# The first chunk of an expert FFN, worked tile by tile as its rows are gathered

## The chip, the cores and the metric

One NeuronCore of one Trainium2 chip runs the kernel. The metric is the device time of a launch in microseconds (us); before the change it is 1994.89 us, the median of 3 runs (1994.32 to 1996.13). Engines are called TensorE (matmuls; in the profile PE, and PEld for its weight loads), VectorE (DVE), ScalarE (ACT), GpSimd (POOL) and SyncE (SP, which here only starts DMAs).

## The reference, cut to what matters

The layer is a "macaron": half an expert FFN, an attention, half an expert FFN again, over 8192 tokens of width 256, all in float32.

```python
x = x + 0.5 * ffn(layernorm(x), router_w, wg, wu, wd)
x = x + attn(layernorm(x), Wq, bq, Wk, bk, Wv, bv, Wo, bo)
x = x + 0.5 * ffn(layernorm(x), router_w, wg, wu, wd)
```

In the FFN each token goes to its two best of 8 experts. An expert takes at most 1280 tokens (those of highest weight), and computes for its gathered rows `disp` (unused places are rows of zeros):

```python
g = einsum('ecd,edf->ecf', disp, wg)
u = einsum('ecd,edf->ecf', disp, wu)
eo = einsum('ecf,efd->ecd', silu(g) * u, wd)     # D = 256, F = 1024
```

The results, weighted, are added back to the tokens' rows. The change touches only how the first gathered rows of each FFN reach the first products.

## The kernel before, in words

The program runs four stages in order: the first router (which norms the rows, chooses experts and writes the rows with their weights to DRAM), the first FFN (`experts`, from L452), attention with the second router, and the second FFN (`experts` again). In both FFNs the code is the same.

**Chunks.** An expert's 1280 places are worked in two chunks of 640, each made of `CH` = 5 tiles of 128 rows; an FFN has 16 chunks. For each chunk, `gather` (L464) starts five indirect DMAs from GpSimd's queue, each bringing a tile `r` of 128 rows. `blank` (L477) multiplies a tile by 0 or 1 per row, on ScalarE, or on VectorE for tiles 1 and 3 of chunk 0. `turn` (L487) transposes one half of the width (`c`, 0 or 1) of tiles 0 to 2 or of tiles 3 and 4 into the PSUM bank `tr`, and ScalarE copies the bank to `xsT`; four calls (`q` = 0 to 3: c 0 tiles 0-2, c 0 tiles 3-4, c 1 tiles 0-2, c 1 tiles 3-4) turn a chunk.

**Products.** The first and second matrices of the expert, `wg` (m = 0) and `wu` (m = 1), are multiplied by a Strassen-like scheme: the inner width of 256 is split in two (c), the 640 columns in two halves of `BH` = 320, the 1024 outputs in two halves, and seven products of 128x128 weights with 320 columns replace eight, for each of `NF` = 4 groups `p` of outputs. `sums_of_x` (L544) makes the four sums of column blocks that the scheme needs (`xs`), on VectorE; `sums_of_w` and `sum_of_wd` make those of the weights. A product's result takes a pair of PSUM banks (`banks`, tag `mm`, three pairs in rotation), one bank for m = 0 and one for m = 1. Each float32 matmul in the code is two instructions on TensorE in the profile; a transpose is one.

For one p: the first product (block 11 of the weights by block 11 of x) is copied by ScalarE to `p1`; the second product is added to it in PSUM (for p = 0 of chunk 0 it goes to a pair of its own, and VectorE adds the two into block 0 of `ct`); the sixth product, added to `p1`, gives `u2` (u in the profile), and the following products lead to the other blocks. Then SiLU, the multiplication of the two halves, and in `down` (L749) the third matrix.

**Order.** The stage runs under a schedule written by hand: on TensorE, VectorE and ScalarE the instructions run in the order in which the code emits them. Only GpSimd's order is left to the planner. In the middle of an FFN a chunk's blanks and turns are placed between the products of the chunk before it. The first chunk has none before it, and its start is written out: after the list of rows is made (`first`, L835 to L843), `gather(0)`, `gather(1)`, the sums of the weights on VectorE, then blanks of tiles 0 to 2, turns 0 and 2, blanks of tiles 3 and 4 (L848 to L851), and then, in `units(0)` (L559), the first product, turn 1, half the second product, turn 3, the other half (L623 to L631), the four sums of x, and the addition of the two products (L633). After that come the sum of `wd` (L635), the sixth product with the addition that makes u (L610 to L615, L636), another sum of `wd`, and the loop over p.

The lines in the profile that matter here: L471 the gathers, L483 and L485 the blanks, L496 transposes, L499 copies to `xsT`, L502 all VectorE additions by `tt` (told apart by their tiles: xs, ct, u, wds, ws), L570 the products, L607 the copy to p1.

Of the kernel before, what the change touches and what calls it, by code (L numbers as in the profile page):

```python
# [8 lines left out]
F32 = mybir.dt.float32  # L9
# [4 lines left out]
ALU = mybir.AluOpType  # L14
# [4 lines left out]
P = 128  # L19
# [7 lines left out]
def macaron_kernel(  # L27
# [22 lines left out]
    nc = tc.nc  # L50
    B, N, D = x_in.shape
# [3 lines left out]
    DC = D // P  # L55
# [3 lines left out]
    CH = 5  # L59
    BANK = 512  # L60
# [21 lines left out]
    ident = const.tile([P, P], F32, name="ident")  # L82
# [353 lines left out]
    def load_expert(e, wpool, weights):  # L436
        if e >= E:
            return
        wgt = wpool.tile([P, DC, F], F32, tag="wgt", name="wgt")
        wut = wpool.tile([P, DC, F], F32, tag="wut", name="wut")  # L440
        wdt = wpool.tile([P, FC, D], F32, tag="wdt", name="wdt")
        nc.sync.dma_start(out=wgt, in_=wg[e].rearrange("(c p) f -> p c f", p=P))
        nc.sync.dma_start(out=wut, in_=wu[e].rearrange("(c p) f -> p c f", p=P))
        nc.sync.dma_start(out=wdt, in_=wd[e].rearrange("(f p) d -> p f d", p=P))
        weights[e] = wgt, wut, wdt
# [3 lines left out]
    BH = CH * P // 2  # L449
    TURN = 3  # L450

    def experts(name, src, dst, wait_for, weights, wpool, pool, ppool):  # L452
# [8 lines left out]
        lists, got, xTs, turned, ws, wds, xs = {}, {}, {}, {}, {}, {}, {}  # L461
        sent = {-1: list(wait_for)}

        def gather(k):  # L464
            if k >= len(chunks):
                return
            e, i0 = chunks[k]
            got[k] = []
            for i in range(i0, i0 + CH):
                r = pool.tile([P, W], F32, tag="r", name="r", bufs=10)  # L470
                nc.gpsimd.indirect_dma_start(  # L471
                    out=r, out_offset=None, in_=src[:, :],
                    in_offset=bass.IndirectOffsetOnAxis(ap=lists[e][:, i : i + 1], axis=0),
                )
                got[k].append(r)

        def blank(k, *tiles):  # L477
            for i in tiles:
                if k < len(chunks):
                    e, r = chunks[k][0], got[k][i]  # L480
                    has = r[:, D + E + e : D + E + e + 1]
                    if k == 0 and i % 2:
                        nc.vector.tensor_scalar(r[:, 0:D], r[:, 0:D], has, None, ALU.mult)  # L483
                    else:
                        nc.scalar.mul(r[:, 0:D], r[:, 0:D], has)  # L485

        def turn(k, q):  # L487

            if k >= len(chunks):
                return  # L490
            if q == 0:
                turned[k] = xTs[k] = pool.tile([P, DC, CH * P], F32, tag="xsT", name="xsT", bufs=2)
            c, i0, i1 = q // 2, (0, TURN)[q % 2], (TURN, CH)[q % 2]
            ps = ppool.tile([P, BANK], F32, tag="tr", name="tr", bufs=1)
            for i in range(i0, i1):
                nc.tensor.transpose(  # L496
                    ps[:, (i - i0) * P : (i - i0 + 1) * P], got[k][i][:, c * P : (c + 1) * P], ident
                )
            nc.scalar.copy(turned[k][:, c, i0 * P : i1 * P], ps[:, : (i1 - i0) * P])  # L499

        def tt(o, a, b, op):
            nc.vector.tensor_tensor(o, a, b, op)  # L502

# [3 lines left out]
        def sums_of_w(e, m):  # L507

            if e >= E:
                return  # L510
            if m == 0:
                ws[e] = pool.tile([P, 2, 4, FH], F32, tag="ws", name="ws", bufs=1)
            v, o = weights[e][m], ws[e]
            a11, a12, a21, a22 = v[:, 0, :FH], v[:, 1, :FH], v[:, 0, FH:], v[:, 1, FH:]
            tt(o[:, m, 0, :], a21, a22, ALU.add)
            tt(o[:, m, 1, :], o[:, m, 0, :], a11, ALU.subtract)
            tt(o[:, m, 2, :], a11, a21, ALU.subtract)
            tt(o[:, m, 3, :], a12, o[:, m, 1, :], ALU.subtract)

        def sum_of_wd(k, j):  # L520


            if k % PER:
                return
            e = chunks[k][0]
            v = weights[e][2]
            if j == 0:
                wds[e] = pool.tile([P, 4, NF, P], F32, tag="wds", name="wds", bufs=1)
            o = wds[e]
            a11, a12, a21, a22 = v[:, :NF, :P], v[:, NF:, :P], v[:, :NF, P:], v[:, NF:, P:]  # L530
            of = ((a21, a22, ALU.add), (o[:, 0], a11, ALU.subtract), (a11, a21, ALU.subtract),
                  (a12, o[:, 1], ALU.subtract))
            tt(o[:, j], *of[j])
# [10 lines left out]
        def sums_of_x(k):  # L544
            if k >= len(chunks):
                return
            v = turned.pop(k)
            o = xs[k] = pool.tile([P, 4, BH], F32, tag="xs", name="xs", bufs=1)
            b11, b12, b21, b22 = v[:, 0, :BH], v[:, 0, BH:], v[:, 1, :BH], v[:, 1, BH:]
            tt(o[:, 0, :], b12, b11, ALU.subtract)  # L550
            tt(o[:, 1, :], b22, o[:, 0, :], ALU.subtract)
            tt(o[:, 2, :], b22, b12, ALU.subtract)
            tt(o[:, 3, :], b21, o[:, 1, :], ALU.subtract)

        def banks():

            return ppool.tile([P, 2, BANK], F32, tag="mm", name="mm", bufs=3)

        def units(k):  # L559
            e = chunks[k][0]  # L560
            xT, hs = xTs.pop(k), []

            def product(p, m, ps, j, c, b, start=True):


                if c is None:
                    a = ws[e][:, m, j, p * P : (p + 1) * P]
                else:
                    a = weights[e][m][:, c, j * FH + p * P : j * FH + (p + 1) * P]
                nc.tensor.matmul(ps, a, b, start=start, stop=True, skip_group_check=not start)  # L570

            def both(p, *what):
                ps = banks()
                for m in range(2):
                    product(p, m, ps[:, m, :BH], *what)
                return ps[:, :, :BH]
# [8 lines left out]
            cts, firsts, sixths, u2s = {}, {}, {}, {}  # L585
# [7 lines left out]
            def block(p, q):  # L593

                return cts[p][:, :, q, :]
# [7 lines left out]
            def first_product(p):  # L603

                ps = both(p, 0, 0, xT[:, 0, :BH])
                p1 = pool.tile([P, 2, BH], F32, tag="p1", name="p1", bufs=1)
                nc.scalar.copy(p1, ps)  # L607
                firsts[p] = ps, p1
# [8 lines left out]
            def second_product(p):  # L617
                cts[p] = pool.tile([P, 2, 4, BH], F32, tag="ct", name="ct", bufs=NF)
                c11 = onto(p, firsts.pop(p)[0], 0, 1, xT[:, 1, :BH])
                nc.scalar.activation(h(p)[:, 0, :], c11[:, 0, :], AF.Silu)  # L620
                nc.scalar.copy(hT(p)[:, 0, :], c11[:, 1, :])

            first_product(0)  # L623
            if k == 0:

                turn(0, 1)
                cts[0] = pool.tile([P, 2, 4, BH], F32, tag="ct", name="ct", bufs=NF)
                ps = banks()
                product(0, 0, ps[:, 0, :BH], 0, 1, xT[:, 1, :BH])
                turn(0, 3)  # L630
                product(0, 1, ps[:, 1, :BH], 0, 1, xT[:, 1, :BH])  # L631
                sums_of_x(0)
                tt(block(0, 0), firsts[0][1], ps[:, :, :BH], ALU.add)  # L633
            x4 = xs.pop(k)
            sum_of_wd(k, 0)  # L635
            sixth_product(0)  # L636
            sum_of_wd(k, 1)
            if k > 0:
                second_product(0)
            send(k - 1, 2, 3)  # L640
            for p in range(NF):
                last = p == NF - 1
                u2, ps = u2s.pop(p), sixths.pop(p)
# [192 lines left out]
        with tc.manual_schedule(engines=ENGINES - {mybir.EngineType.Pool}):  # L836
            first.high()
            first.begin()
            for g in range(NL):
                first.low(g)  # L840
                first.products(g)
            first.sum()
            lists[0] = first.end()  # L843
            gather(0)
            gather(1)
            for m in range(2):
                sums_of_w(0, m)
            blank(0, *range(TURN))  # L848
            for q in (0, 2):
                turn(0, q)  # L850
            blank(0, *range(TURN, CH))  # L851
            for k, (e, i0) in enumerate(chunks):
                (down if k < len(chunks) - 1 else down_at_once)(k, units(k))
                if i0 + CH == ST:
                    load_expert(e + 2, wpool, weights)
# [379 lines left out]
    with tc.tile_pool(name="w1", bufs=2) as wpool:  # L1235
        weights = {}
        with tc.tile_pool(name="r1", bufs=1) as pool, tc.tile_pool(name="r1p", bufs=2, space=PSUM) as ppool:
# [5 lines left out]
            with tc.manual_schedule(engines=ENGINES):  # L1243
                nc.gpsimd.memset(wrx, 0.0)
                ps = ppool.tile([P, DC, P], F32, tag="turn", name="wrT", bufs=1)
# [4 lines left out]
                ps = ppool.tile([P, DC, P], F32, tag="turn", name="means", bufs=1)  # L1250
# [74 lines left out]
```

## Time and profile before

| | us |
|---|---|
| median of 3 runs | 1994.89 |
| the profiled execution | 1995.5 |
| its span, first to last instruction | 1993.6 |
| TensorE busy with matmuls | 1832.5 (92%) |
| VectorE busy | 1408.0 (71%) |
| GpSimd busy | 1024.0 (51%) |
| ScalarE busy | 957.9 (48%) |
| mean granted TensorE clock | 0.957 of full |

In the views that follow, times are in us from the first instruction. The chain is followed back from the last instruction, at each step to what released it. "Idle before" is the time in which an engine had nothing running ahead of the instruction, with what ended it. An engine's rows overlap slightly[...]. The first FFN's first tile is blanked at 117.19, the second FFN's at 1205.06.

### The profile page before, as it was taken

To read this page: it belongs to the slowest core of one execution; us is meant where nothing else is said; L and a number is where in the kernel's file an instruction comes from. 1 tells how busy PE (TensorE), PEld (TensorE's weight loads), DVE (VectorE), ACT (ScalarE), POOL (GpSimd) and SP (SyncE) were. 2 spreads that over 40 slices of the span, in tenths; PEclk is the share of its full clock that TensorE was granted. 3 is DMA by queue.
4 is the path that set the end of the run, shared out by engine and by line. 5 is a ranking of instruction groups with operands and counts; after the bars stand their busy time and mean duration, and the time that the engine had idled before them with its cause. 6 is when DMAs were issued, how large, how long until landed. Compare 5 with 4: busy or idle time off the path is not lost.

```text
span 1993.6 us, 25454 instructions
## 1 busy us (share of the span) xinstructions
PE 1832.5 (92%) x8756; PEld 1333.5 (67%) x8756; DVE 1408.0 (71%) x2609; ACT 957.9 (48%) x2373; POOL 1024.0 (51%) x1036
## 2 busy tenths in 40 slices
PE   6369999999999999999999617999999999999998
PEld 4247777777777777777888415777777777777776
DVE  8866767676767676646788886676767676666763
ACT  5435454555546463325455404555546463736332
POOL 5325555555555555535555304555555555555552
PEclk8579999999999999999999858999999999999999
DMA  9901313232222221125012541222222222231121
GB/s 348 318 28 28 91 28 91 37 82 66 53 70 49 70 49 28 28 25 172 22 43 87 173 152 29 50 69 70 49 70 49 70 49 71 49 91 31 31 30 19
DMA packets 99936, 147.67 MB, mean 74 GB/s; under 512 B 7512, under 2 KB 86368, under 8 KB 99680
## 3 DMA queue, kind: packets, MB, share of 16 engines
q1 hardware_dynamic: 69072, 102.77, 15.1%
q0 software_dynamic: 30720, 43.27, 13.5%
q8 instruction: 69, 1.13, 0.2%
q14 instruction: 59, 0.48, 0.1%
q10 hardware_dynamic: 16, 0.01, 0.0%
HBM read 98.84 MB, written 55.57 MB: 77 GB/s over the span
## 4 chain that ended last, share of the span: by engine, by line
PE 82%; DVE 8%; issue 1%; POOL 1%; ACT 1%; DMA 1%; POOLq 0%; DVEq 0%; ACTq 0%; SPq 0%
PE mm L570 48%; PE mm L770 23%; PE tr L496 2%; PE back L722 2%; PE pc L1012 1%; PE qp L957 1%; PE ix L413 1%; PE py L1070 1%; DVE above L309 1%; PE mm L828 1%; DVE st L1082 1%; DVE xw L1080 1%; DVE q L965 1%; DVE m L970 0%; DVE z L979 0%
## 5 line engine op out<-in xcount | busy, mean ns | idle before, releaser
L570 PE MATMUL mm<-xs,ws 128*128 128x320 f32 x1536 | 477.0, 433 | 3.9 <-DVE u L502 3.0
L505 POOL TENSOR_TENSOR ct<-ct 128x320 f32<-128x320 f32 x360 | 338.8, 941 | 188.8 <-DVE ct L601 165.3
L570 PEld LDWEIGHTS mm<-xs,ws 128*128 128x128 f32 x1536 | 284.3, 190 | 113.0 <-DVE u L502 4.1
L502 DVE TENSOR_TENSOR ct<-u,mm 128x640 f32<-128x640 f32 x256 | 209.8, 820 | 180.4 <-PE mm L570 168.0
L502 DVE TENSOR_TENSOR ct<-ct,mm 128x640 f32<-128x640 f32 x288 | 235.9, 819 | 74.3 <-PE mm L570 74.1
L598 ACT ACTIVATE ct<-ct 128x960 f32<-128x960 f32 (+2 forms) x192 | 141.7, 738 | 297.9 <-DVE ct L502 297.9
L471 POOL DMA_INDIRECT r<-rows,ixs x160 | 157.8, 986 | 236.0 <-ACT eo L703 172.9
L770 PE MATMUL mm<-ct,wds 128*128 128x320 f32 x960 | 278.1, 432 | 0.0
L407 ACT ACTIVATE lo<-from_below,behind_lo 128x129 f16<-128x129 f32 x896 | 272.9, 395 | 0.0
L770 PEld LDWEIGHTS mm<-ct,wds 128*128 128x128 f32 x960 | 178.6, 190 | 72.8 <-DVE ct L502 6.0
L770 PE MATMUL mm<-ct,wdt 128*128 128x320 f32 x720 | 213.5, 433 | 0.0
L704 POOL DMA_INDIRECT out_dram<-eo,ixs x80 | 127.6, 1595 | 142.1 <-ACT eo L703 124.5
L704 POOL DMA_INDIRECT acc<-eo,ixs x80 | 127.6, 1595 | 141.9 <-ACT eo L703 124.0
L570 PE MATMUL mm<-xsT,wgt 128*128 128x320 f32 x512 | 183.4, 440 | 0.0
L570 PE MATMUL mm<-xsT,wut 128*128 128x320 f32 x512 | 180.7, 435 | 0.0
L601 DVE TENSOR_TENSOR ct<-ct 128x640 f32<-128x640 f32 (+1 forms) x128 | 165.7, 1295 | 18.7 <-ACT ct L598 18.7
L502 DVE TENSOR_TENSOR u<-p,mm 128x640 f32<-128x640 f32 x128 | 105.1, 821 | 88.2 <-PE mm L570 81.0
L770 PEld LDWEIGHTS mm<-ct,wdt 128*128 128x128 f32 x720 | 132.1, 190 | 47.5
L607 ACT COPY p<-mm 128x640 f32<-128x640 f32 x128 | 88.3, 690 | 154.5 <-PE mm L570 154.5
L570 PE MATMUL mm<-xsT,ws 128*128 128x320 f32 x512 | 158.7, 432 | 0.0
L703 ACT ACTIVATE eo<-back,r 128x256 f32<-128x256 f32 x150 | 65.0, 478 | 152.4 <-PE back L722 152.4
L570 PEld LDWEIGHTS mm<-xsT,wut 128*128 128x128 f32 x512 | 97.7, 191 | 40.7 <-issue 0.8
(226 smaller groups left out, 2836.9 us busy)
## 6 DMA issues: line engine op xcount, KB each, us to landing
wgt<-in_L_ffn_wg_dram SPq DMA_DIRECT2D x16, 1024.0 KB, 4.9
wut<-in_L_ffn_wu_dram SPq DMA_DIRECT2D x16, 1024.0 KB, 6.9
wdt<-in_L_ffn_wd_dram SPq DMA_DIRECT2D x16, 1024.0 KB, 5.3
rows<-xw SPq DMA_DIRECT2D x7, 2176.0 KB, 10.7
xw<-in_L_attn_x_dram SPq DMA_DIRECT2D x16, 512.0 KB, 8.2
out_dram<-xw SPq DMA_DIRECT2D x16, 512.0 KB, 2.9
xw<-acc SPq DMA_DIRECT2D x15, 512.0 KB, 8.8
r<-rows,ixs POOLq DMA_INDIRECT x160, 2.8
```

The source lines that it names most:

```text
L407: nc.scalar.activation(lo[:, t, :], from_below, AF.Sign, bias=at, scale=1.0)
L471: nc.gpsimd.indirect_dma_start(out=r, out_offset=None, in_=src[:, :], in_offset=bass.IndirectOffsetOnAxis(ap=lists[e][:, i : i + 1], axis=0),)
L496: nc.tensor.transpose(ps[:, (i - i0) * P : (i - i0 + 1) * P], got[k][i][:, c * P : (c + 1) * P], ident)
L502: nc.vector.tensor_tensor(o, a, b, op)
L505: nc.gpsimd.tensor_tensor(o, a, b, op)
L570: nc.tensor.matmul(ps, a, b, start=start, stop=True, skip_group_check=not start)
L598: nc.scalar.activation(h(p)[:, qs, :], h(p)[:, qs, :], AF.Silu)
L601: engine.tensor_tensor(h(p)[:, qs, :], h(p)[:, qs, :], hT(p)[:, qs, :], ALU.mult)
L607: nc.scalar.copy(p1, ps)
L703: nc.scalar.mul(eo, ps, got[k][i][:, D + e : D + e + 1])
L704: ins = nc.gpsimd.indirect_dma_start(out=dst[:, :], out_offset=bass.IndirectOffsetOnAxis(ap=lists[e][:, i0 + i : i0 + i + 1], axis=0), in_ ...
L770: nc.tensor.matmul(ps, a(p), b(p), start=(p == 0 and not more), stop=(p == NF - 1), skip_group_check=more)
```

## The change

For chunk 0 alone, the order is turned round. Each of the five tiles is blanked, then transposed whole: both halves of its width go into the one `tr` bank by two transposes, and one ScalarE copy of 256 columns takes them to `xsT` (`turn_tile`). As soon as a tile is there, its columns are multiplied: of the first 320 columns, tile 0 gives 128, tile 1 gives 128 and tile 2 gives 64, and for each of these groups the first product (c = 0, into `ps`) and the second product (c = 1, into `ps2`, a pair of banks of its own) are made, both for m = 0 and 1. After tile 2, ScalarE copies `ps` to `p1`. Tiles 3 and 4 are only blanked and turned. The sums of x stand after all five tiles. The addition of the two products into block 0 moves behind the sixth product, its addition u, and the second sum of `wd`. Other chunks are as before.

```diff
+        def turn_tile(k, i):
+            ps = ppool.tile([P, BANK], F32, tag="tr", name="tr", bufs=1)
+            for c in range(DC):
+                nc.tensor.transpose(ps[:, c * P : (c + 1) * P], got[k][i][:, c * P : (c + 1) * P], ident)
+            nc.scalar.copy(
+                turned[k][:, :, i * P : (i + 1) * P], ps[:, :D].rearrange("p (c s) -> p c s", c=DC)
+            )
...
-            xT, hs = xTs.pop(k), []
+            xT, hs = turned[0] if k == 0 else xTs.pop(k), []
...
-            first_product(0)
             if k == 0:
 
-                turn(0, 1)
                 cts[0] = pool.tile([P, 2, 4, BH], F32, tag="ct", name="ct", bufs=NF)
-                ps = banks()
-                product(0, 0, ps[:, 0, :BH], 0, 1, xT[:, 1, :BH])
-                turn(0, 3)
-                product(0, 1, ps[:, 1, :BH], 0, 1, xT[:, 1, :BH])
+                ps, ps2 = banks(), banks()
+                for i in range(CH):
+                    blank(0, i)
+                    turn_tile(0, i)
+                    at = slice(i * P, min((i + 1) * P, BH))
+                    for c, o in ((0, ps), (1, ps2)) if i < TURN else ():
+                        for m in range(2):
+                            product(0, m, o[:, m, at], 0, c, xT[:, c, at])
+                    if i == TURN - 1:
+                        p1 = pool.tile([P, 2, BH], F32, tag="p1", name="p1", bufs=1)
+                        nc.scalar.copy(p1, ps[:, :, :BH])
+                        firsts[0] = None, p1
                 sums_of_x(0)
-                tt(block(0, 0), firsts[0][1], ps[:, :, :BH], ALU.add)
+            else:
+                first_product(0)
             x4 = xs.pop(k)
             sum_of_wd(k, 0)
             sixth_product(0)
             sum_of_wd(k, 1)
-            if k > 0:
+            if k == 0:
+                tt(block(0, 0), p1, ps2[:, :, :BH], ALU.add)
+            else:
                 second_product(0)
...
-            blank(0, *range(TURN))
-            for q in (0, 2):
-                turn(0, q)
-            blank(0, *range(TURN, CH))
+            turned[0] = pool.tile([P, DC, CH * P], F32, tag="xsT", name="xsT", bufs=2)
```

## The prediction

> **What bounds the kernel now.** I read the page first, then the chain that ended last in order of time, then the order of time at the two places that the change touches, then windows that show TensorE's granted clock. TensorE carries the kernel:
>
> ```profile
> PE 1832.5 (92%) x8756; PEld 1333.5 (67%) x8756; DVE 1408.0 (71%) x2609; ACT 957.9 (48%) x2373; POOL 1024.0 (51%) x1036
> ...
> PE 82%; DVE 8%; issue 1%; POOL 1%; ACT 1%; DMA 1%; POOLq 0%; DVEq 0%; ACTq 0%; SPq 0%
> PE mm L570 48%; PE mm L770 23%; PE tr L496 2%; PE back L722 2%; PE pc L1012 1%; PE qp L957 1%; PE ix L413 1%; PE py L1070 1%; DVE above L309 1%; PE mm L828 1%; DVE st L1082 1%; DVE xw L1080 1%; DVE q L965 1%; DVE m L970 0%; DVE z L979 0%
> ```
>
> Inside an FFN the chunks follow each other at TensorE's pace, so a microsecond won or lost before the first chunk's steady part moves the end by as much. The change touches only that start, once in each FFN. The chain there (start, duration, what):
>
> ```profile
> 117.18 2.83 DMA r<-rows,ixs
> ...
> 121.64 0.90 PE tr L496 x3
> 122.54 2.15 PE mm L570 x4
> ...
> 124.71 0.69 ACT p L607
> 125.40 0.28 ACT xsT L499
> ...
> 126.21 0.38 ACT xsT L499
> ...
> 126.61 1.29 DVE xs L502 x3
> 127.91 0.73 DVE ct L502
> 128.64 0.60 DVE wds L502
> 129.24 0.74 DVE u L502
> ```
>
> TensorE's unbroken work begins at 130.03, 12.84 us after tile 0 is blanked at 117.19. In the second FFN it is 1205.06 to 1218.11, 13.05 us. At stake are these two stretches, 26 us, of which the last tile's landing (about 122.5: its gather ends at 120.68, and tiles 1 to 3 land some 1.8 after theirs) can't be moved. To see what a product costs there (start, duration, engine, line, idle time before):
>
> ```profile
> 117.76 0.48 PE L496 MATMUL tr<-ident,r 128*128 128x128 f32 x1 [5.37 <-ACT r L485]
> ...
> 122.34 1.27 PE L570 MATMUL mm<-xsT,wgt 128*128 128x320 f32 x2
> ...
> 124.82 0.70 PE L570 MATMUL mm<-xsT,wgt 128*128 128x320 f32 x2
> ```
>
> One product in the code is two instructions. 320 columns at the low clock take 2.15/4 = 0.54 each, at the full one 0.27. For 128 columns there is a row elsewhere, eight instructions at the full clock:
>
> ```profile
> 1008.21 1.05 PE L1046 MATMUL ctx<-gT,wvx 128*128 128x128 f32 x8
> ```
>
> With 0.27 of drain that is (1.05-0.27)/7 = 0.11 each; at the half clock 0.215. The clock itself, from windows (length, PE busy, PEld, DVE, ACT, POOL, granted clock, DMA):
>
> ```profile
> 117.90:121.31 3.41, 1.29 (x3) 0.40 (x3) 0.49 (x3) 0.71 (x2) 2.50 (x4) 0.50 0.33 102
> 121.31:124.72 3.41, 3.08 (x9) 2.17 (x10) 0.29 (x1) 1.17 (x4) 2.51 (x3) 0.50 0.44 123
> 124.72:128.14 3.42, 2.76 (x12) 1.45 (x10) 2.02 (x5) 2.89 (x9) 1.99 (x2) 1.00 0.37 102
> 128.14:131.55 3.41, 1.89 (x8) 1.13 (x7) 2.58 (x5) 0.79 (x3) 0.00 (x0) 1.00 0.05 20
> 59.87:63.28 3.41, 2.51 (x9) 1.60 (x10) 2.97 (x12) 1.21 (x4) 2.23 (x5) 0.50 0.69 211
> 950.75:954.16 3.41, 1.29 (x10) 1.02 (x10) 3.10 (x10) 3.15 (x7) 2.12 (x2) 1.00 0.00 0
> ```
>
> After 3.08 busy us in a window the clock rose; after 2.51 (59.87) it stayed low. After 1.29 (950.75) it fell in the next window; after 1.89 (128.14) it held.
>
> [...] ScalarE's rows here keep the written order. [...] 0.11 is the pitch at 128 columns. So I take 64 columns to be no cheaper than 128, an estimate, with half as the other end (0.4 us less per FFN).
>
> **The change part by part.** ScalarE is strictly in the written order: blank 0, copy 0, copy 1, blank 2, copy 2, p1, copy 3, blank 4, copy 4. TensorE: transposes 0, products 0, transposes 1, and so on. Removed: four products of 320 columns and copies of 384, 384, 256, 256 columns (0.48, 0.48, 0.38, 0.37). Added: twelve products (24 instructions) of 128, 128 and 64 columns, and five copies of 256 columns (0.38 each). No DMA moves, the gathers on POOL's queue stand as before, SP has nothing here.
>
> The first tiles are worked at the half clock. Tile 0: blanked 117.70, transposed 118.44, copied 118.84; products begin at 118.89: 0.21 for the first weight load, exposed by the wait, and 8 x 0.215 = 1.72, so TensorE is free at 120.82. Tile 1, blanked at 119.12, now queues behind these: transposed 121.45, copied 121.84. Blank 2, ready to start at 120.01, stands behind copy 1 in ScalarE's queue and ends at 122.25.
>
> If the clock rises at 121.31, one window earlier than now: products 1 from 121.89 (0.11 + 8 x 0.11 = 0.99) to 122.88; transposes 2 end 123.26, copy 2 123.66, products 2 123.70 to 124.69. ps is complete at about 124.35, so p1 runs 124.40 to 125.09 (0.69), copy 3 behind it to 125.48, blank 4 behind that to 125.89 though its tile landed at 122.5, transposes 4 to 126.38, copy 4 to 126.78. Before, the last copy ended at 126.59: +0.19.
>
> From there the end of the start: the four sums now all wait for the last copy (the first began early, at 125.71): +0.41. The addition into block 0 leaves its place ahead of u: -0.73. Otherwise as before, sixth product begins 0.55 after the second sum starts, and u follows its 1.34: 126.80 + 0.41 + 0.55 + 1.34 + 0.02 = 129.12 for u, and 0.87 later, as now, 129.99 for TensorE, against 130.03. The wds sum before u (0.60) is covered by the sixth product; without it u would be that much later. The moved addition ends at about 131.3 and frees its banks for the fifth product, which TensorE reaches at 130.0 + 8 x 0.27 = 132.2: 0.9 to spare. With one accumulating pair of banks replaced by two, nothing waits for a bank.
>
> So this part is worth 0.0. By clock: were all of it at full clock from 117.9 (excluded here, the array was idle the window before), the same chain gives copy 4 at 125.30, -1.5 per FFN. If the clock rises only at 124.72 as now, products 1 take until 123.82, products 2 run 124.90 to 125.89, copy 4 ends 127.97: +1.15.
>
> Then the tail. From 124.7 to 130.0 TensorE has only transposes 3 (0.4), 4 (0.44) and the sixth product (1.34). The window 124.72 to 128.14 would hold 0.35 + 0.44 + 0.38 = 1.17 busy us, less than the 1.29 after which the clock fell; before it held 2.76. A fall for 128.14 to 131.55 slows three sixth-product instructions by 0.27 each (0.81) and the steady work after by about 0.35: +1.15; if the next window, busy some 70%, doesn't lift it, until 134.96: +2.9. Where the windows lie better, nothing.
>
> The second FFN's windows lie 1 us later from its tile 0 (1210.16, 1213.58): rise there at 122.3 of the first FFN's times gives +0.14, less its own 0.21 in the 13.05: -0.1, and its tail window holds about 1.6: a toss-up, 0 or +1.3.
>
> Sum: 0.0 + 1.15 - 0.1 + half of 1.3 gives +1.7; with some weight on a late rise, +2.0. The profiled execution took 1995.5 (span 1993.6, 1.9 around it); the median 1994.89 is 0.6 below. On the median: 1996.9.
>
> **Rivals.**
> 1. Gain: the clock rises early and holds, 64 columns are cheap, the shortened tail counts in full: -0.25 to -1.5 per FFN, total -0.5 to -3: about 1993.4. For it: u moves up 0.73, products start 3.4 us earlier. Against it: ScalarE's order, p1 and copy 3 ahead of blank 4.
> 2. Slower: the half clock stays through the whole start. Place: products 0 to 2, where each tile has 1.72 us of products in a period of about 3.0. [...] It decides if the rise needs more than that; in the records, 74% busy was not enough and 90% was. Price: products 1 to 123.82, products 2 to 126.83, copy 4 to 129.38, sixth product 1.1 slower, TensorE at 133.8, and up to 1.7 in the first steady window: +3.8 to +5.5 per FFN, 2002.5 to 2005.9; in one FFN alone, about 2000.
> 3. The change makes no difference because the transfers set the pace: the last landing at 122.5 would have to be on the chain; blank 4 follows it by 2.9 us. I give this no chance apart from the likeliest case.
>
> **How the numbers follow.** Likeliest, 0.60: two starts worth 0 to +1.75 each, 1994.9 to 1998.4, at 1996.9. Rival 2 in one or both, 0.25: 1999 to 2006. Rival 1, 0.12: 1992 to 1994.8. Something unseen and faster, 0.03. A range with 0.08 below and 0.12 above: 1993.2 to 2001.5. This kernel's measurement can tell 0.2%, 4 us, from no change: faster 0.03, same 0.72, slower 0.25.
>
> **What would show it.** Right: transposes 1 start behind products 0 (some 1.6 us later than 119.18 did); blank 4 directly behind copy 3; PE idle before the sixth product waiting for xs; u right after the sixth product; clock 0.50 in a window near the first steady products. Wrong: last xsT copy before 125.5 from the same tile 0, or products 1 begun before 121.

## The result, and the profile after

The changed kernel takes 2003.72 us (median of 6 runs, 1999.36 to 2007.44) against 1994.91 for the kernel before (6 runs, 1993.22 to 1996.13): ratio 1.0042, 95% interval 1.0033 to 1.0052. It is slower, by 8.8 us between the medians, outside the range given. The profiled execution took 2007.44 with a span of 2005.6, 12.0 more than the span before.

Of the page's busy times only TensorE's differs much from before: it is 11.6 us longer, close to what the execution lost, with 32 more instructions. The shares of the chain hardly differ:

```profile
PE 1844.1 (92%) x8788; PEld 1342.7 (67%) x8788; DVE 1409.0 (70%) x2609; ACT 958.8 (48%) x2375; POOL 1024.8 (51%) x1036
...
PE 83%; DVE 8%; issue 1%; ACT 1%; POOL 1%; DMA 1%; POOLq 0%; DVEq 0%; ACTq 0%; SPq 0%
```

The chain at the start of the first FFN, in order of time (start, duration, what). Tile 0 is now blanked at 117.86, 0.67 later than before:

```profile
119.57 2.08 PE mm L578 x8
121.65 0.44 PE tr L504 x2
...
122.53 2.08 PE mm L578 x8
...
125.50 1.97 PE mm L578 x8
127.47 0.44 PE tr L504 x2
...
127.94 0.37 ACT xsT L505
128.31 0.42 ACT r L485
...
128.77 0.70 PE tr L504 x2
...
129.90 0.50 DVE xs L510
...
130.97 2.51 PE mm L578 x4
...
133.51 0.83 DVE u L510
...
134.39 5.62 PE mm L578 x10
```

This is one serial walk from tile to tile, with 2.08 us (the third time 1.97) for the eight instructions of a product group, and 2.51 for the sixth product where it was 1.34 before: TensorE is at half speed throughout. The steady products begin at 134.39, 16.53 us after tile 0 (12.84 before), and run at half speed too: ten instructions in 5.62. The windows say the same. They are 3.41 us long, and every change of the clock in this trace falls on one of their borders (those at 115.92, 139.81, 1119.43 and 1122.85 lie 7, 287 and 1 such lengths apart). Each row has length, PE busy, PEld, DVE, ACT, POOL, granted clock and DMA:

```profile
119.33:122.74 3.41, 2.71 (x11) 2.31 (x12) 0.71 (x2) 0.82 (x3) 2.59 (x3) 0.50 0.45 123
122.74:126.16 3.42, 2.96 (x13) 2.56 (x14) 0.00 (x0) 0.52 (x2) 2.72 (x3) 0.50 0.39 111
126.16:129.57 3.41, 2.43 (x11) 1.63 (x10) 0.00 (x0) 1.55 (x4) 1.07 (x2) 0.50 0.34 98
129.57:132.98 3.41, 2.00 (x4) 1.17 (x4) 2.39 (x5) 2.65 (x9) 0.00 (x0) 0.50 0.00 0
132.98:136.40 3.42, 2.51 (x5) 1.43 (x5) 2.15 (x3) 0.00 (x0) 0.00 (x0) 0.50 0.00 0
136.40:139.81 3.41, 3.41 (x7) 2.11 (x7) 1.57 (x2) 0.00 (x0) 0.00 (x0) 0.50 0.00 0
139.81:143.22 3.41, 3.41 (x14) 2.42 (x13) 1.90 (x4) 1.49 (x2) 0.00 (x0) 1.00 0.00 0
```

The fullest window of the tile loop holds 2.96 us of TensorE work and the clock stays at 0.50 after it; it rises only after a window of unbroken steady products (3.41 us), 22 us after tile 0 (7.5 before).

**Where the time went.** I measured each trace from the blank of tile 0 to the start of the 40th product instruction behind the first steady one, which takes the clock's late rise in:

| kernel | first FFN | second FFN | sum against before |
|---|---|---|---|
| before | 23.81 | 24.02 | 47.83 |
| after | 30.17 | 29.85 | +12.2 |

The two starts are 12.2 us longer, the whole execution 12.0; the rest of both FFNs agrees within 0.4 us each, and what stands around and between the FFNs is 0.8 shorter in sum. Of the 12.2, 3.70 and 3.48 are the later beginning of the steady products, and 2.66 and 2.35 are what their first 40 instructions take longer, the first 5 us of them at half speed. The median run lost less than the profiled one, which was the slowest of the six. A second profile of the same kernel (after_again, below) shows one way in which executions differ: there the clock rose for one window inside the first tile loop.

### The profile page after: what moved, and what is told of

It is laid out like the page before. It is cut to its first block, busy times and chain, and to the rows that moved or that the text cites. A ratio compares the mean times of both kernels' runs of the same rounds, so it can differ in the third digit from the quotient of the medians.

```text
span 2005.6 us, 25520 instructions
## 1 busy us (share of the span) xinstructions
PE 1844.1 (92%) x8788; PEld 1342.7 (67%) x8788; DVE 1409.0 (70%) x2609; ACT 958.8 (48%) x2375; POOL 1024.8 (51%) x1036
## 4 chain that ended last, share of the span: by engine, by line
PE 83%; DVE 8%; issue 1%; ACT 1%; POOL 1%; DMA 1%; POOLq 0%; DVEq 0%; ACTq 0%; SPq 0%
PE mm L578 49%; PE mm L787 23%; PE tr L496 2%; PE back L739 2%; PE qp L971 1%; PE pc L1026 1%; PE ix L413 1%; PE py L1084 1%; DVE above L309 1%; PE mm L845 1%; DVE st L1096 1%; DVE xw L1094 1%; DVE q L979 1%; DVE m L984 0%; DVE z L993 0%
## 5 line engine op out<-in xcount | busy, mean ns | idle before, releaser
L578 PE MATMUL mm<-xs,ws 128*128 128x320 f32 x1536 | 482.2, 437 | 4.9 <-DVE xs L510 3.0
L578 PE MATMUL mm<-xsT,wgt 128*128 128x320 f32 (+2 forms) x528 | 187.6, 438 | 2.8 <-ACT xsT L505 2.8
L578 PE MATMUL mm<-xsT,wut 128*128 128x320 f32 (+2 forms) x528 | 184.4, 432 | 0.0
L578 PEld LDWEIGHTS mm<-xsT,wut 128*128 128x128 f32 x528 | 102.3, 196 | 39.9
```

## The experiments

**Theory clock:** the change lost its time because the start, cut into short groups with waits for ScalarE between them, no longer holds a window full enough to raise TensorE's clock, and so the whole start and the first steady products run at half speed. **Theory order:** the chain itself became too long at any clock, through ScalarE's queue (p1 and copy 3 ahead of blank 4) and the round trips per tile. The kernels ran in three groups, each on one chip: w_after, w_before, whole and ct_later; gap_mm, gap_tr, hot_after and best; after_again, after_early, after_tail and whole_tail. Each ratio is against the kernel before on the same chip, which took 1998.2 us in the first group, 1998.4 in the second and 1994.9 in the third. The times expected for the first group were written for 1994.9, so they are to be compared as ratios. The changed kernel itself ran on the third group's chip and in the first measurement, not on the other two chips.

### Filling TensorE's idle time (w_after, w_before)

```diff
             lists[0] = first.end()
+            warm = ppool.tile([P, BANK], F32, tag="one", name="warm", bufs=1)
+            stay_busy(warm, 4)
...
                     turn_tile(0, i)
+                    if i >= TURN:
+                        stay_busy(warm, i - TURN + 1, 256)
...
             sixth_product(0)
+            if k == 0:
+                stay_busy(warm, 1, 256)
```

In `w_before` the fillers stand in the kernel before: the same four, one of 256 columns behind each of the first three transposes, one of 512 behind the sixth product. `stay_busy` multiplies constants into a bank that nobody reads.

> The changed kernel with matmuls on constants put into TensorE's idle time at each FFN's start: four of 512 columns while the gathers are under way, and one or two of 256 columns behind the transposes of tiles 3 and 4 and behind the sixth product. They add work and take no wait away. Theory clock (the time was lost because no window of the start is full enough to raise the clock): TensorE runs the whole start at full speed, the steady products begin some 5 us sooner per FFN, 1990 to 1994 us, below the kernel before. Theory order (the chain between ScalarE, TensorE and VectorE is too long at any clock: blank 4 behind copy 3 behind p1): little is won, 2001 to 2004 us.

> The kernel before with the same four matmuls on constants ahead of tile 0, one of 256 columns behind each of the first three transposes, and one of 512 behind the sixth product. Theory clock: the four instructions of the first product run at 0.27 instead of 0.54, the clock no longer moves with the place of the window, 1.0 to 1.8 us per FFN, 1991.5 to 1993 us. Theory order: nothing moves, 1994.9 us within 1.

Measured: w_after 1998.55 us, ratio 1.0004 (0.9996 to 1.0013); w_before 1995.54 us, ratio 0.9986 (0.9980 to 0.9993). Work was added, no wait was taken away, and of the changed kernel's 0.42% only 0.04% is left. That is what theory clock says and theory order can't. But the fillers helped the kernel before too, and filled against filled the new order is still 3.0 us slower. So most of the loss goes with the clock, and up to 3 us of some 8 do not. Nor did w_after come out below the kernel before, as theory clock had expected. One reason is in its windows: in the first FFN the clock, full at first, fell in the thin tail. (The tail is the stretch behind the first two products, in which TensorE has only the transposes of tiles 3 and 4, the sixth product and here the fillers.)

```profile
118.81:122.22 3.41, 2.62 (x20) 2.28 (x20) 0.71 (x2) 1.05 (x3) 2.73 (x3) 1.00 0.42 112
122.22:125.63 3.41, 2.16 (x16) 1.63 (x15) 0.00 (x0) 1.84 (x4) 2.50 (x4) 1.00 0.42 108
125.63:129.05 3.42, 3.42 (x9) 2.21 (x8) 2.42 (x5) 2.72 (x9) 1.39 (x2) 0.50 0.38 111
```

In its second FFN the clock held at 1.00 throughout, and the steady products began 12.36 us after tile 0. The filled kernel before needed 11.32 and 11.44, with the clock at 1.00 all through; the largest part of its gain is in the row of first products, 1.09 for four instructions where it was 2.15:

```profile
122.67 1.09 PE mm L572 x4
```

So at one clock the new order was not ahead of the old one.

### Undoing one part: products undivided (whole)

```diff
-                    at = slice(i * P, min((i + 1) * P, BH))
-                    for c, o in ((0, ps), (1, ps2)) if i < TURN else ():
+                    at = slice(0, BH)
+                    for c, o in ((0, ps), (1, ps2)) if i == TURN - 1 else ():
```

> The changed kernel with the products not divided by columns: tiles still turned one by one, but both products made in 320 columns after tile 2. Theory clock: eight instructions of 0.54 in one unbroken stretch raise the clock as before the change, restart some 0.7 us later than before because transposes 3 stand behind all products: 1995 to 1998 us. Theory order: p1, copy 3 and blank 4 stand as in the changed kernel, so at least half of the loss stays: 1999 us or more.

Measured: 2004.6 us, ratio 1.0034 (1.0021 to 1.0048): the number that theory order had expected, not theory clock's. The trace shows what the clock did (windows):

```profile
120.06:123.47 3.41, 2.88 (x6) 1.80 (x7) 0.35 (x1) 0.39 (x2) 2.50 (x4) 0.50 0.35 96
123.47:126.89 3.42, 2.87 (x7) 1.47 (x5) 0.00 (x0) 1.21 (x3) 2.30 (x3) 0.50 0.39 112
126.89:130.30 3.41, 1.58 (x6) 0.88 (x6) 2.18 (x5) 2.88 (x10) 0.00 (x0) 1.00 0.15 41
130.30:133.71 3.41, 2.50 (x5) 1.51 (x5) 2.37 (x4) 0.10 (x1) 0.00 (x0) 0.50 0.02 5
```

The long products did raise the clock, as expected, but the window after that, with the transposes of tile 4 and the sixth product alone, held 1.58 us of work; the clock fell, and the steady products, from 131.50, ran at half speed until 137.12. My expectation left the tail out. Most of the loss stayed although no product was cut, so the cutting alone does not make it. What whole and the changed kernel share is that all first and second products stand ahead of the transposes of tiles 3 and 4, where the kernel before had the second product between and behind these transposes.

### The tail alone (whole_tail, after_tail), and the kernel itself once more (after_again)

```diff
             lists[0] = first.end()
+            warm = ppool.tile([P, BANK], F32, tag="one", name="warm", bufs=1)
...
                     turn_tile(0, i)
+                    stay_busy(warm, 2 if i == CH - 1 else 0, 2 * P)
...
             sixth_product(0)
+            if k == 0:
+                stay_busy(warm, 1, 256)
```

> The kernel with undivided products (label whole: 0.34% over) with the same matmuls on constants in its tail. There the clock rose 8 to 10 us after tile 0 and fell again 3.4 us later, in the tail. Theory clock: with a filled tail it holds, 40 instructions are done about 25.8 us after tile 0 instead of 27.6 to 28.6, 0.05% to 0.15% over the kernel before. Theory order: 0.34% or more.

> The changed kernel with matmuls on constants in the thin tail alone: two of 256 columns behind the transposes of tile 4, one behind the sixth product. At the half clock they take 1.7 and 0.9 us and may delay the chain by some 0.3 each. Theory clock: the tail's windows become full, the clock rises 14 to 18 us after tile 0 instead of 21 to 22, and the first steady products run at full speed: 2 to 3 us less per FFN, 0.1% to 0.25% over the kernel before. Theory order: no gain, 0.42% or more.

> The changed kernel itself once more, unedited, for the comparison with the next three on one chip. Both theories: about 0.42% over the kernel before, steady products 16.5 us after tile 0, clock at 0.50 until some 21 us after tile 0.

Measured: whole_tail 1998.57 us, ratio 1.0017 (1.0010 to 1.0024), half of the loss of whole, which ran on another chip; after_tail 2003.67 us, 1.0041 (1.0028 to 1.0054); after_again 2006.13 us, 1.0045 (1.0029 to 1.0061). In whole_tail the window that had let the clock fall now holds 2.34 us of work, and the clock stays:

```profile
125.26:128.67 3.41, 2.34 (x11) 1.34 (x10) 0.59 (x2) 1.90 (x7) 1.60 (x2) 1.00 0.44 123
```

Its starts are 24.85 and 25.50 long against 28.59 and 27.60, 5.8 us less; 2.8 and 1.4 of it lie in the first 40 steady instructions, which now run at full speed. Not all of the first FFN's part is due to the added work: the clock rose 7.8 us after tile 0 there, ahead of any filler, and 10.2 in whole. In the second FFN it rose later than in whole (8.9 against 7.9), and 2.1 us were won all the same. In after_tail the filled window raised the clock 14.4 us after tile 0 (20.7 in after_again's trace):

```profile
128.30:131.72 3.42, 3.42 (x9) 2.32 (x10) 2.36 (x5) 2.72 (x9) 0.00 (x0) 0.50 0.02 6
131.72:135.13 3.41, 2.93 (x12) 1.90 (x11) 2.64 (x5) 0.00 (x0) 0.00 (x0) 1.00 0.00 0
```

Its starts sum to 54.40 us in the trace, after_again's to 58.73: 4.3 less, as theory clock had it. But the time, 0.41% over, is the one that theory order had expected. The medians differ by 2.5 us and the intervals overlap, so for after_tail the time shows no gain for certain; only the trace does.

after_again, the changed kernel once more, kept the clock low through the start in its second FFN only, where the steady products began 16.53 us after tile 0. In its first FFN the clock rose 7.0 us after tile 0 and fell again one window later:

```profile
120.32:123.73 3.41, 2.95 (x13) 2.32 (x12) 0.35 (x1) 0.78 (x2) 2.58 (x3) 0.50 0.42 102
123.73:127.14 3.41, 1.92 (x13) 1.29 (x12) 0.00 (x0) 1.94 (x5) 2.14 (x3) 1.00 0.38 108
127.14:130.56 3.42, 2.06 (x4) 1.17 (x4) 2.39 (x5) 2.60 (x9) 0.00 (x0) 0.50 0.15 41
```

So an early rise was within this kernel's reach, and little was won by it: the steady products began 15.19 us after tile 0, at half speed, and this start is 28.86 long, 5.0 more than before.

The twelve runs of the changed kernel (six in each measurement) spread from 1999.21 to 2008.50 us, and they do so with the granted clock: it is 0.950 to 0.953 in the seven runs of 2005.05 us and more, 0.954 and 0.955 in the two at 2002, 0.956 or 0.957 in the three of 1999.21 to 1999.36. The kernel before on the third group's chip had 0.956 to 0.958. So even the runs with as high a clock are some 4 us slower than it, which fits the part that the fillers left.

### ScalarE's order (after_early)

```diff
                 for i in range(CH):
-                    blank(0, i)
+                    if i < TURN:
+                        blank(0, i)
                     turn_tile(0, i)
+                    if i == TURN - 1:
+                        blank(0, *range(TURN, CH))
```

> The changed kernel with the blanks of tiles 3 and 4 emitted right behind the turn of tile 2, so ahead of p1 and copy 3 in ScalarE's queue. Theory order: blank 4 leaves the chain and most of the loss goes, 0.1% to 0.2% over the kernel before. Theory clock: the chain is shorter by 0.4 us per FFN (the blank's 0.42 between copy 3 and transposes 4), the clock still stays low, about 0.38% over.

Measured: 2006.14 us, ratio 1.0050 (1.0038 to 1.0062); the steady products begin 16.12 us after tile 0 in both FFNs. Against the 16.53 of the changed kernel that is the 0.4 expected, and blank 4 has left the chain (chain in order of time):

```profile
127.03 0.38 ACT xsT L505
127.41 0.04 issue
127.46 0.70 PE tr L504 x2
```

The time shows nothing of it: the ratio is no better than after_again's. ScalarE's queue, where theory order saw most of the loss, is a small term. The round trips per tile stand unchanged in this run.

### What raises the clock: short gaps filled (gap_mm, gap_tr)

```diff
                     turn_tile(0, i)
+                    stay_busy(warm, 1, P)
```

and for `gap_tr`, in the place of `stay_busy`, two transposes of constants.

> The changed kernel with one matmul on constants, 128 columns (two instructions of 0.215 at the half clock), behind the two transposes of every tile, where TensorE waits for ScalarE's copy; nothing ahead of tile 0. Theory clock [...]: the windows over tiles 0 to 2 now hold enough matmul work (some 2.2 of each 3.0 us instead of 1.7) and the clock rises at the end of the first full one, 4 to 7 us after tile 0; it may fall once in the thin tail; 1998 to 2002 us on the chip where the kernel before takes 1998. Theory order, or a threshold above this: the clock stays at 0.50 until the steady products, 2005 us or more.

> The same with two transposes of constants (two instructions of 0.215 at the half clock) in the place of the matmul. If transposes do not count for the clock, it stays at 0.50 through the start as in the changed kernel, about 8 us over the kernel before. If they count as matmuls do, it rises as with the matmuls.

Measured: 2011.14 us, ratio 1.0068 (1.0055 to 1.0082), and 2011.41 us, 1.0067 (1.0053 to 1.0081): worse than the changed kernel on its own chips. gap_mm's time is the one expected of a clock that stays low, 2005 us or more, but in both the clock rose early, in gap_mm 4.2 and 6.5 us after tile 0, in gap_tr 7.0 and 5.1, and fell again in the tail, to rise for good only after 20 to 22 us. gap_tr's windows:

```profile
117.19:120.60 3.41, 2.99 (x13) 2.59 (x14) 0.87 (x2) 0.70 (x2) 2.64 (x3) 0.50 0.45 123
120.60:124.01 3.41, 3.38 (x16) 2.97 (x16) 0.35 (x1) 0.78 (x2) 2.65 (x3) 0.50 0.41 105
124.01:127.42 3.41, 1.94 (x15) 1.46 (x13) 0.00 (x0) 1.06 (x2) 2.08 (x3) 1.00 0.36 103
127.42:130.84 3.42, 1.40 (x5) 1.00 (x6) 1.32 (x4) 2.54 (x9) 0.00 (x0) 0.50 0.15 42
```

2.99 us of work was not enough, 3.38 was, with transposes as filling. Of the 3.38, the products are 2.28; in the changed kernel's window from 122.74 they are 2.53 of 2.96, and the clock stayed. So transposes count for something. All four starts of the two kernels rose in the loop; of the eight of the changed kernel (both profiles), after_early and after_tail, one did. That the fillers made the difference is likely and not fully shown, since the chip differs too: in hot_after (below), on the chip of these two, the clock also rose once in the loop, 5.0 us after tile 0, with no filler there. An early rise was worth little with a thin tail behind it: the starts of gap_tr are 12.4 us longer than before, those of the changed kernel 12.2. The times of these two hold something else besides: waits that nothing in the profile explains, such as 2.12 us between p1 and copy 3 in gap_mm,

```profile
126.54 2.12 another core or an unknown queue
```

so their distance to the changed kernel is not put down to the clock.

### One edit of the change alone, and the filled kernels once more (ct_later, hot_after, best)

`ct_later` is the kernel before with one edit:

```diff
-                tt(block(0, 0), firsts[0][1], ps[:, :, :BH], ALU.add)
+                ps2, p1 = ps, firsts[0][1]
...
-            if k > 0:
+            if k == 0:
+                tt(block(0, 0), p1, ps2[:, :, :BH], ALU.add)
+            else:
                 second_product(0)
```

> The kernel before with one edit of the change alone: the addition of the first two products into block 0 stands behind u and the second sum of wd. Both theories: u begins 0.73 us sooner, 1.5 us over two FFNs, 1993.4 us; if this edit is part of the loss, 1996 us or more.

Measured: 1997.77 us, ratio 0.9996 (0.9988 to 1.0005). In the trace the steady products begin 12.13 and 12.34 us after tile 0, 0.70 and 0.71 sooner than before, as worked out; over two FFNs 1.4 us lie inside the interval.

`hot_after` is w_after without the filler behind the transposes of tile 3; `best` is w_before with the edit of ct_later and 256 columns for 512 behind the sixth product.

> The changed kernel with four matmuls on constants of 512 columns ahead of tile 0, two of 256 behind the transposes of tile 4 and one behind the sixth product, none behind those of tile 3 (there the copy waited for it). Where the clock holds, the steady products begin 11.3 to 11.8 us after tile 0 (13.0 before the change); if the change's order is as good as the order before it at one clock, within 0.4 us of the 11.4 that the filled kernel before took.

> The filled kernel before with the addition into block 0 moved behind u: steady products 10.7 us after tile 0 in both FFNs, clock at 1.00 throughout; about 4 us below the kernel before, ratio 0.998. If the gains do not add, 0.9986 as with the fillers alone.

Measured: hot_after 1999.89 us, ratio 1.0007 (0.9998 to 1.0015); its clock fell in both FFNs, 1.6, 11.9 and 8.4 us after tile 0, so the comparison at one clock that I wanted was not had; the one to go by is w_after's second FFN. In the second FFN of both, copy 3 starts some 0.6 us after p1, although transposes 3 had ended before p1 did; in hot_after:

```profile
1216.28 0.69 ACT L645 COPY p<-mm 128x640 f32<-128x640 f32 x1 [0.75 <-PE mm L578]
1217.62 0.37 ACT L505 COPY xsT<-tr 128x256 f32<-128x256 f32 x1 [0.65 <-PE tr L504]
```

hot_after has no filler behind transposes 3, so the filler is not the cause of that wait, against what I had expected.

best 1996.13 us, ratio 0.9990 (0.9982 to 0.9998): below the kernel before, no better than w_before. Its first FFN began the steady products after 10.91 us, near the 10.7 expected, the second after 12.46. There VectorE waited for the sixth product, whose last instruction ended at about 1216.0, until 1217.35, which the profile doesn't explain:

```profile
1217.35 0.82 DVE L504 TENSOR_TENSOR u<-p,mm 128x640 f32<-128x640 f32 x1 [1.32 <-PE mm L572]
```

### All starts side by side

From the blank of tile 0 to the start of the 40th instruction behind the first steady one, us, from one trace each, with the ratio of the times:

| kernel | first | second | sum against before | ratio |
|---|---|---|---|---|
| after | 30.17 | 29.85 | +12.2 | 1.0042 |
| after_again | 28.86 | 29.87 | +10.9 | 1.0045 |
| after_early | 29.39 | 29.57 | +11.1 | 1.0050 |
| after_tail | 26.97 | 27.43 | +6.6 | 1.0041 |
| whole | 28.59 | 27.60 | +8.4 | 1.0034 |
| whole_tail | 24.85 | 25.50 | +2.5 | 1.0017 |
| gap_mm | 30.42 | 29.05 | +11.6 | 1.0068 |
| gap_tr | 29.75 | 30.47 | +12.4 | 1.0067 |
| w_after | 23.80 | 23.34 | -0.7 | 1.0004 |
| hot_after | 26.26 | 24.07 | +2.5 | 1.0007 |
| ct_later | 23.10 | 23.32 | -1.4 | 0.9996 |
| best | 21.89 | 23.44 | -2.5 | 0.9990 |
| w_before | 22.29 | 22.41 | -3.1 | 0.9986 |

## Why the prediction was wrong

**The step that failed** is "If the clock rises at 121.31, one window earlier than now", taken for the likeliest case. It rested on the tile loop's windows being full enough, and the records of before left that open: 74% busy had not raised the clock, 90% had. The prediction never worked out its own window from 117.90 to 121.31: by its times, transposes 0 (0.54), products 0 (1.93) and transposes 1 (0.49) put about 2.96 us into it, 87%, between the two. The loop's windows came to 2.71 and 2.96 us of 3.41, 79% and 87%, and the clock stayed. The second FFN's fullest held 2.93. The sum's terms that hung on an early rise, 0.0 to 1.75 per FFN, were void. What happened in the profiled execution is the second rival, given 0.25, in both FFNs. It was a near thing: in after_again's first FFN a window of 2.95 us did raise the clock. But the tail then lost it, and that start was 5.0 us longer than before, where the likeliest case allowed 0 to 1.75.

**That rival's working held, up to its last term.** Taken from tile 0, it put the end of copy 4 at 129.38 and TensorE's restart at 133.8; the trace, 0.67 later throughout, has 129.87 and 134.39, so 129.20 and 133.72. Products 0, put at 1.93 with 0.21 for the first weight load, held TensorE for 1.87, from 119.57 to the transposes at 121.44: eight steps of 0.21, and 0.16 ahead of the second instruction. The mis-sized term is the steady work at half speed, "up to 1.7": it measured 2.66 and 2.35, because the first steady window was not full either (2.51 us in 132.98 to 136.40: u's wait lies in it) and the rise came a whole window later. That makes 6.4 and 5.8 per FFN in the profiled execution where 3.8 to 5.5 was written. The median run lost 8.8 in all, 4.4 per FFN, inside that rival's numbers; which FFNs of that run had a low clock is not known.

**The thin tail** was seen, as a possible fall of the clock for 1.15 to 2.9 us. In the changed kernel's first profile it never came to that, since the clock had not risen. In after_again's first FFN, in whole and in gap_tr it did fall there. What that cost can be read from whole against whole_tail: 2.8 and 1.4 us in the first 40 steady instructions of the two FFNs.

**Right:** transposes 1 stood behind products 0; blank 4 ran directly behind copy 3, and was worth 0.4 (after_early); the addition moved behind u was worth 0.70 (ct_later) and held up no bank; 64 columns were no cheaper than 128, which had been an estimate without a row of 64 columns behind it. These two rows of the changed kernel, in order of time, start 0.43 apart, two instructions each, as the rows of 128 columns do (120.16, 120.58, 121.01):

```profile
126.41 0.63 PE L578 MATMUL mm<-xsT,wgt 128*128 128x64 f32 x2
...
126.84 0.63 PE L578 MATMUL mm<-xsT,wut 128*128 128x64 f32 x2
```

All five signs named for "right" came true, and neither of those for "wrong". Four are signs of the order of the work, which the likeliest case and the second rival share, and the fifth, a half clock near the first steady products, fits both; none tells whether the clock rises early.

**The gain at full clock** was put at 1.5 per FFN, and excluded because TensorE had been idle the window before (in the trace of before, 0.14 us of work in 114.49 to 117.90, and a granted clock of 0.50 in the window that followed). w_after's second FFN, with the clock at 1.00 throughout, began its steady products after 12.36 us instead of 13.05, 0.7 less; the 0.6 us by which copy 3 started late, a wait that the profile doesn't explain, is part of what is missing. The old order at that clock took 11.3 to 11.4. What the change sets out to win, earlier products, is won more fully by the clock alone.

**Still open:** what exactly is counted for the rise. In whole a window with 2.87 us of recorded TensorE work raised the clock, and the one before it, with 2.88, didn't; with the short products 2.95 did (after_again) and 2.96 didn't (the changed kernel). I counted all windows of the 14 profiled executions: at the half clock none up to 2.82 us (83%) raised it and every one from 3.06 (90%) on did; in between both occur. The prediction's case stood in that gap. That the spread of the changed kernel's runs goes with the granted clock is measured for each run; that the place of the windows makes it is argued from two profiles. And the 3 to 4 us that the new order loses beside the clock are not traced to a single wait.

## What to carry to other kernels

Starting a matmul's pieces as their inputs landed cost more here than the overlap won (0.42%): the work came in short groups, 2.08 us of products and 0.88 until the next, with a round trip to ScalarE between them, and it left the stretch behind it thin, 2.00 us of TensorE work in the 3.41 from 129.57. TensorE's granted clock was part of the path: the 40 instructions from the first steady one took 2.66 and 2.35 us longer for its late rise. It must be read, window by window, before and after. Where the start had idle TensorE time anyway, matmuls on constants there were worth 0.14% (w_before), without any change of order. A filled loop was not enough: in gap_tr the clock rose after a window of 3.38 us, fell after the next, of 1.94, and rose for good only 20 to 22 us after tile 0.

## What the runs showed of the hardware that I had not expected

- The clock went to full and back to half within one window of 3.41 us (whole, 126.89 to 130.30), so this early rise was lost at once. There it fell after 1.58 us of work in a window, and held after 2.34 in whole_tail. No one figure divides the two: in the 14 profiled executions every full-clock window of more than 2.19 us (64%) held the clock and every one under 1.42 (42%) lost it, and in between both occur (1.89 held in the kernel before, 2.16 fell in w_after).
- With transposes of constants in the gaps (gap_tr) the clock rose early in both FFNs, as it did with matmuls there (gap_mm), once after a window of 3.38 us of which the products were 2.28. Whether transposes count for the clock had been open; here they counted for something (a window of 2.96 us with 2.53 of products did not raise it in the changed kernel), and no run measures how much.
- The first two groups ran on chips on which the kernel before takes 1998.2 to 1998.4 us, 3.4 more than in the other runs. The steady part of each FFN measured 756.0 to 756.7 us there (all eight traces) and 754.3 to 754.8 elsewhere, 3.4 us over two FFNs. Waits of 1 to 2 us that the profile gives no reason for appear in these traces (in ct_later VectorE's ct additions wait 30.4 us for "issue" in sum, 10.9 before). Their cause stays open.
